# A graph layer: twelve single rows per step instead of twenty-four, fourteen gathers instead of twelve

## The chip, the core and the metric

The kernel runs on one core of a Trainium2 chip. The metric is the device time of one execution in microseconds, less is better. Three executions of the kernel before took 17983.56, 17994.12 and 17994.94 us; the median is 17994.12.

## The reference

One layer of a graph network with two kinds of edges, a residual sum and a layer norm. There are 50000 nodes with 128 features (f32), and 1650000 edges: 800000 random pairs in both directions and one self-loop per node. They are sorted by `dst`; `src` is random.

```python
Xs = X[src]
m_data = Xs @ W_data.T + b_data
m_ctrl = Xs @ W_control.T + b_control
msg = jnp.where((edge_types == 0)[:, None], m_data, m_ctrl)
agg = jax.ops.segment_sum(msg, dst, num_segments=X.shape[0])
out = jax.nn.relu(agg + (X @ W_self.T + b_self))
x = _layernorm(x + out, axis=-1)
```

The matrices can be applied after the sum: per node it is enough to have the sum of its neighbours' rows for each kind of edge, and how many edges of each kind there are.

## The kernel before, in words

**Blocks and steps.** `straight` walks the sorted edges in NBLK = 514 blocks. All blocks but the first and the last hold BE = 3212 edges, in Q = 2 steps of 1606. The edges of a step come in by three ways:

- R = 12 *gathers* of 128 edges (L536). GpSimd issues an indirect DMA, which fetches 128 rows of x, one per partition, into a slot of the tile `y`. Each gather's column of indices is in `idx`.
- F = 46 *fillers*. In the gathers, an edge whose source is its own destination (a self-loop) needs no fetch, since that row is loaded for the block anyway. `columns` counts the loops per gather and ranks them; `fill` (L349 to L378) writes the next filler edges into the places of the loops and makes the new indices. What is left over is passed to the next step (`late`, the serial chain at L323, up to LATE = 10 edges); FX = 56 is F plus these. `by` holds which nodes' loops were taken out; the `left_out_` functions (L380 to L409) build a matrix from it and put the loops' own rows back.
- S = 24 *single rows*. Each is a DMA of its own with one row of 512 bytes, its address in a register (L510); SP issues 12 and ScalarE 12 per step (TURNS), so 48 per block, 24576 in all. They are issued after the first pass of a block, for the block two further on, into the tile `yx`.

The first block and the last have gathers only (24 and 19), so that there are 24 + 512 x 24 + 19 = 12331 gathers.

**Sums.** For each gather, TensorE multiplies the rows in `y` by a 0/1 matrix `oh` (L467, DVE: 128 x 26 columns of 2W = 120; W = 60 is how many nodes a step may span, once for each kind of edge) and adds up in PSUM (`acc`, L555). The matrix of a step's single rows is the thirteenth column (L561). `cnt` (L475, DVE) is the sum of `oh` over the gathers and gives the counts (L564). `add` (L569, DVE) adds a step's `acc` to the block's `sums` at an address in a register, `begin_sums` (L571) takes over the overlap with the block before. `layer` (L582 to L591) multiplies a finished block of B = 112 nodes by the matrices, `moments`, `root` and `store` (L593 to L622) do the norm, and SP writes the rows (L626).

**Order.** The order is written out by hand (`manual_schedule`); every engine works its instructions off in this order, and tiles are given back through semaphores. A block's 24 gathers are four *passes* of PASS = 6. `y` has SLOTS = 10 slots, each for one pass: `gathers` (L530) gives a pass to GpSimd, and TensorE waits until the pass has landed (L543). GpSimd may issue the pass after next ten only when TensorE is done with the slot's last use.

Around the four passes of a block (L682 to L735): ahead of the first pass come `spread` for the block to be filled (L347, TensorE), the add of the last block's second step, `begin_sums`, `onehot` and `counts` for the block two further on (AHEAD). After the first pass come `left_out_columns` (L384, TensorE, reads `by`) and `fill` for a block up to five further on (RAHEAD); after the second the layer of the block before, the loops' rows and the moments; after the third, in the second block of each group of GB = 10, `columns` for the next group.

**Beginning and end.** Ahead of the loop (L661 to L681) the numbers of all blocks (L205 to L223), `columns(0)`, `fill(1)` and `fill(2)` are made. The last block is treated like the others; `find_bad` runs at its beginning and finds out whether the data kept the bounds that the kernel assumes (else a general version runs). After the loop come the last two stores.

Of the kernel before, what the change touches and what calls it, by code (L numbers as in the profile page):

```python
# [12 lines left out]
F32 = mybir.dt.float32  # L13
# [14 lines left out]
P = 128  # L28
# [6 lines left out]
R = 12  # L35
W = 60
Q = 2
PASS = 6
B = 112
C = R * Q  # L40
F = 46
LATE = 10
FX = LATE + F
TURNS = (12, 12)
# [37 lines left out]
GS = GB * Q  # L82
SPAN = 8
# [14 lines left out]
def straight(ctx, tc, c, x, x_t, edges_t, edges_f, src_x, dst_first, first_p, out):  # L98
# [62 lines left out]
    row_of = keep.tile([GB, GB], BF16, name="row_of")  # L161
    nc.vector.tensor_copy(row_of, c["ident"][:GB, :GB])
# [41 lines left out]
    nc.vector.tensor_tensor(begin_p, begin_p, base_p, op=ALU.add)  # L204
    wide = keep.tile([1, WG, SPAN], F32, name="wide")  # L205
    bases_f = keep.tile([1, WG * SPAN], F32, name="bases_f")
    nc.vector.memset(bases_f, float(N - B))
    nc.vector.tensor_copy(bases_f[:, :NBLK], base[0:1, :NBLK, 0])
    first_of_span = bases_f.rearrange("o (w s) -> o w s", s=SPAN)
    nc.vector.tensor_scalar(wide, first_of_span[:, :, 0:1].to_broadcast([1, WG, SPAN]), float(N - WIDE), None, op0=ALU.min)  # L210
    within = keep.tile([1, WG, SPAN], F32, name="within")
    nc.vector.tensor_tensor(within, first_of_span, wide, op=ALU.subtract)
    at_i = keep.tile([1, WG * SPAN, 4], I32, name="at_i")
    nc.vector.tensor_copy(at_i[:, :NBLK, :Q], begin[0:1, :NBLK, :])
    nc.vector.tensor_scalar(at_i[:, :, 3], within.rearrange("o w s -> o (w s)"), 0.0, float(WIDE - B), op0=ALU.max, op1=ALU.min)
    nc.vector.tensor_tensor(begin, begin, base.to_broadcast([P, BL, Q]), op=ALU.add)
    base_i = keep.tile([1, WG, 2 * SPAN], I32, name="base_i")
    nc.vector.tensor_scalar(base_i[:, :, 0], wide[:, :, 0], 4.0, None, op0=ALU.mult)
    nc.vector.tensor_scalar(base_i[:, :, 1:1 + SPAN], first_of_span, float(ROW), None, op0=ALU.mult)
    shift = keep.tile([1, NBLK], F32, name="shift")  # L220
    nc.vector.memset(shift, 0.0)
    nc.vector.tensor_tensor(shift[:, 1:], base[0:1, 1:NBLK, 0], base[0:1, :NBLK - 1, 0], op=ALU.subtract)
    nc.vector.tensor_scalar(at_i[:, :NBLK, 2], shift, 0.0, float(B), op0=ALU.max, op1=ALU.min)  # L223


# [10 lines left out]
    def columns_of(d, t, first, name):  # L236

        rel = eds.tile(list(d.shape), F32, name="rel" + name, bufs=1)
# [3 lines left out]
        nc.vector.tensor_scalar(col, t, 0.0, float(W), op0=ALU.not_equal, op1=ALU.mult)  # L242
        nc.vector.tensor_tensor(col, col, rel, op=ALU.add)
        return col, rel
# [8 lines left out]
    def packed(src, col):  # L253

        lim = eds.tile(list(col.shape), F32, name="lim", bufs=1)
        nc.vector.tensor_scalar(lim, col, 0.0, float(COLS - 1), op0=ALU.max, op1=ALU.min)
        v = eds.tile(list(col.shape), F32, name="v")
        nc.vector.scalar_tensor_tensor(v, src, float(COLS), lim, op0=ALU.mult, op1=ALU.add)
        return v

    def columns(g):
# [27 lines left out]
        col, rel = columns_of(a["d"], a["t"], first_of, "")  # L289
        check(a["d"], rel, [stats[:, 0, m, g:g + 1] for m in range(2)], "")  # L290
        col_f, rel_f = columns_of(a["df"], a["tf"], first_of_f, "_f")
# [5 lines left out]
        with nc.allow_low_precision(reason="whole numbers below 256 times a power of two"):  # L297
            nc.vector.tensor_scalar(v_f[:, 0, :], col_f, 0.0, float(COLS - 1), op0=ALU.max, op1=ALU.min)
            lo = eds.tile([GB, Q * FX], F32, name="lo", bufs=1)
            nc.vector.scalar_tensor_tensor(lo, hi, -float(COLS), a["sf"], op0=ALU.mult, op1=ALU.add)  # L300
            nc.vector.tensor_scalar(v_f[:, 1, :], lo, float(COLS), None, op0=ALU.mult)
            nc.vector.tensor_scalar(v_f[:, 2, :], hi, float(COLS * COLS), None, op0=ALU.mult)

        cb = eds.tile([P, GB, C1], F32, name="cb")
        nc.vector.tensor_scalar(cb, a["t"], 0.0, float(P), op0=ALU.not_equal, op1=ALU.mult)
        nc.vector.tensor_tensor(cb, cb, a["d"], op=ALU.add)
# [8 lines left out]
        more = eds.tile([P, GS], F32, name="more", bufs=1)  # L315
        nc.vector.tensor_scalar(more, rank[:, :, R], -1.0, float(F), op0=ALU.mult, op1=ALU.add)
        late = eds.tile([P, GS + 1], F32, name="late")
        if g == 0:
            nc.vector.memset(late, 0.0)
        else:  # L320
            nc.vector.tensor_copy(late[:, 0:1], late_g[g - 1][:, GS:])
        for k in range(at, n):
            nc.vector.tensor_scalar(late[:, k + 1:k + 2], more[:, k:k + 1], late[:, k:k + 1], 0.0,  # L323
                                    op0=ALU.add, op1=ALU.max)
# [5 lines left out]
        if n < GS and g > 0:  # L330
            nc.vector.memset(late[:, n + 1:], 0.0)
# [8 lines left out]
    def spread(b):  # L340

        if plain(b):
            return
        g, i = divmod(b, GB)
        vf = lists[b % 2][:, :Q * FX]
        for m in range(3):
            nc.tensor.matmul(vf, row_of[:, i:i + 1].to_broadcast([GB, P]), vp_g[g][:, m, :], start=m == 0, stop=m == 2)  # L347
# [71 lines left out]
    def steps_of(b):  # L419
        return [q for q in range(Q) if len(chunks_of(b, q))]  # L420

    def passes_of(b):

        for p in range(C // PASS):
            q = p * PASS // R
            yield q, [k for k in chunks_of(b, q) if k // PASS == p]

# [36 lines left out]
    def onehot(b):  # L464
        g, i = divmod(b, GB)
        oh = ohp.tile([P, C1, 2 * W], F32, name="oh")
        nc.vector.tensor_tensor(oh, col_g[g][:, i, :, None].to_broadcast([P, C1, 2 * W]),  # L467
                                num_ps[:, None, :].to_broadcast([P, C1, 2 * W]), op=ALU.is_equal)
        ohs[b] = oh

    def counts(b):

        cnt = ohp.tile([P, Q, 2 * W], BF16, name="cnt")
        with nc.allow_low_precision(reason="whole numbers up to R1"):
            nc.vector.tensor_reduce(cnt, ohs[b].rearrange("p (q r) w -> p q w r", r=R1), AX.X, ALU.add)  # L475
        cnts[b] = cnt
# [105 lines left out]
    def layer(b):  # L582
        a = sums[b % RING]
# [3 lines left out]
        nc.tensor.matmul(po, xT, c["wselfT"], start=True, stop=False)  # L587
        nc.tensor.matmul(po, a[0:3, 2, :B], bias, start=False, stop=False)  # L588
        for t in range(2):
            nc.tensor.matmul(po, a[:, t, :B], c["wmsgT"][:, t * D:(t + 1) * D], start=False, stop=t == 1)  # L590
        pos[b] = both  # L591

    def moments(b):  # L593
        h = stp.tile([B, D], F32, name="h", bufs=4)
        po = pos.pop(b)
        nc.vector.tensor_copy(h, po[:, 1, :])  # L596
        nc.vector.scalar_tensor_tensor(h, po[:, 0, :], 0.0, h, op0=ALU.max, op1=ALU.add)  # L597
        st = stp.tile([B, 6], F32, name="st")
        nc.vector.bn_stats(st, h)  # L599
        if b % 2 == 0:  # L600
            mvs[b // 2] = stp.tile([B, 2, 2], F32, name="mv")
        mv = mvs[b // 2][:, b % 2, :]
        nc.vector.bn_aggr(mv, st)
        hs[b] = h

    def pair(b):

        return range(b // 2 * 2, b + 1) if b % 2 == 1 or b == NBLK - 1 else ()

    def root(bs):  # L610
        sd = stp.tile([B, 2], F32, name="sd")
        nc.scalar.activation(sd[:, :len(bs)], mvs[bs[0] // 2][:, :len(bs), 1], AF.Sqrt, bias=c["eps"][:B, :])
        sds[bs[0] // 2] = sd

    def store(bs):
        mv = mvs.pop(bs[0] // 2)
        rstd = stp.tile([B, 2], F32, name="rstd")
        nc.vector.reciprocal(rstd[:, :len(bs)], sds.pop(bs[0] // 2)[:, :len(bs)])
# [41 lines left out]

    for b in range(1, AHEAD + 1):  # L661
        offsets(b)
    columns(0)
    window(0)
    spread(1)
    fill(1)
# [3 lines left out]
    onehot(0)  # L670
    counts(0)
# [10 lines left out]
    for b in range(NBLK + 1):  # L682
        if b == NBLK - 1:
            find_bad()
# [5 lines left out]
        due, fresh = fresh, range(made + 1, min(b + RAHEAD, made + 2, NBLK - 1) + 1)  # L690
# [5 lines left out]
        if b < NBLK:  # L696
            begin_sums(b)
# [5 lines left out]
        for q, (step, ks) in enumerate(passes_of(b)):  # L703
# [21 lines left out]
            if q == 2 and i == 1 and g + 1 < GROUPS:  # L725
                columns(g + 1)
# [9 lines left out]
    store(pair(NBLK - 1))  # L736
    for b in (*ready, *pair(NBLK - 1)):
        store_rows(b)
# [338 lines left out]
```

## Time and profile before

| | |
|---|---|
| median of three executions | 17994.12 us |
| the profiled execution | 18008.86 us |
| its span | 18006.8 us |
| GpSimd (POOL) busy | 11686.9 us, 65% |
| VectorE (DVE) busy | 12374.8 us, 69% |
| TensorE matmuls (PE) busy | 8608.7 us, 48% |
| ScalarE (ACT) busy | 79.2 us |
| granted TensorE clock, mean | 0.54 |
| HBM traffic over the span | 50 GB/s |

The span is what the profile records from the first instruction to the last; the profiled execution's own time is 2 us longer, and 15 us above the median of the three executions. A line of a group has the line of the program, the engine, the operation, out<-in with sizes and the number of instructions, then busy time in us and the mean duration in ns, then the idle time of that engine ahead of these instructions, and what ended most of it. A line of the timeline has the start in us, the duration, the instruction, and in brackets the idle time before it and what ended that. Queues (SPq, ACTq, POOLq) are the DMAs that an engine issued. "Remote" is a release that the profile can't put down to an instruction of this core. Idle time of an engine that is not the bottleneck costs nothing.

### The profile page before, as it was taken

What the parts mean: (1) busy time and instruction counts of PE and PEld (TensorE: products, weight loads), DVE (VectorE), ACT (ScalarE), POOL (GpSimd) and SP (SyncE); (2) the same over time, 40 slices, a digit from 0 to 9 for tenths busy, and PEclk for the clock granted to TensorE, in tenths of its full rate; (3) what the DMA queues carried; (4) which work ended last, traced back from release to release, by engine and by line L of the source; (5) the groups of instructions that cost most, each with busy time, mean ns of one, the idle gap of its engine ahead of it and who ended that gap; (6) DMA issues with size and microseconds to landing.
All of it is one profiled execution on the core that took longest, in us unless ns stands there. A gap on an engine that the chain in (4) does not pass through costs nothing.

```text
span 18006.8 us, 165600 instructions
## 1 busy us (share of the span) xinstructions
PE 8608.7 (48%) x37659; PEld 7345.2 (41%) x37660; DVE 12374.8 (69%) x15212; ACT 79.2 (0%) x263; POOL 11686.9 (65%) x12341
## 2 busy tenths in 40 slices
PE   3444444444444444444444444444444444444444
PEld 3344443444344444444444444444444444444444
DVE  7676676676666666666766766676676676667665
ACT  0000000000000000000000000000000000000000
POOL 6666666666666666666666666666666666666666
PEclk6555555555555555555555555555555555555555
DMA  1111111111111111111111111111111111111111
GB/s 52 51 50 51 52 50 51 52 50 51 50 52 51 50 52 50 51 51 51 51 50 52 51 50 51 51 51 51 51 51 50 51 52 50 51 52 50 51 50 48
DMA packets 529272, 913.91 MB, mean 51 GB/s; under 512 B 232762, under 2 KB 315875, under 8 KB 528274
## 3 DMA queue, kind: packets, MB, share of 16 engines
q0 software_dynamic: 394592, 808.89, 15.7%
q1 hardware_dynamic: 108668, 87.80, 1.7%
q10 hardware_dynamic: 25014, 6.54, 0.2%
q8 instruction: 306, 5.01, 0.1%
q14 instruction: 692, 5.67, 0.1%
HBM read 872.82 MB, written 29.47 MB: 50 GB/s over the span
## 4 chain that ended last, share of the span: by engine, by line
DVE 51%; another core or an unknown queue 28%; issue 13%; PE 7%; DVEq 0%; ACTq 0%; ACT 0%
DVE cnt L475 14%; DVE oh L467 8%; PE acc L555 5%; DVE m L358 4%; DVE v_new L365 4%; DVE new L361 4%; DVE old L374 4%; DVE sums L569 2%; DVE late L323 1%; DVE z L392 1%; DVE h L597 1%; DVE st L599 1%; DVE xT L461 1%; DVE h L596 1%
## 5 line engine op out<-in xcount | busy, mean ns | idle before, releaser
L536 POOL DMA_INDIRECT y<-in_x,idx x12312 | 11667.4, 948 | 6272.6 <-issue 3435.2
L555 PEld LDWEIGHTS acc<-oh,y 128*128 128x128 f32 x24662 | 5375.0, 315 | 8665.3 <-issue 8100.0
L555 PE MATMUL acc<-oh,y 128*128 128x120 f32 x24662 | 6002.7, 413 | 3679.8 <-issue 3675.4
L569 DVE TENSOR_TENSOR sums<-acc,sums 128x180 f32 x1028 | 350.0, 340 | 4142.8 <-remote 3960.0
L475 DVE TENSOR_REDUCE cnt<-oh 128x240 bf16<-128x3120 f32 x514 | 3008.2, 5852 | 17.9
L384 PE MATMUL small<-ones_b,by 128*112 128x1 bf16 x512 | 83.5, 164 | 4632.6 <-issue 3934.5
L467 DVE TENSOR_TENSOR oh<-col,small 128x3120 f32<-128x3120 f32 x514 | 1740.8, 3387 | 117.3 <-remote 95.1
L377 DVE TENSOR_REDUCE by<-old 128x112 bf16<-128x1456 f32 x512 | 1427.3, 2788 | 17.4
L358 DVE TENSOR_TENSOR m<-rk,small 128x1456 f32<-128x1456 f32 x512 | 855.7, 1671 | 17.4
L361 DVE TENSOR_TENSOR new<-m,small 128x1456 f32<-128x1456 f32 x512 | 855.2, 1670 | 17.5
L365 DVE TENSOR_REDUCE v_new<-new 128x26 f32<-128x1456 f32 x512 | 855.0, 1670 | 17.5
L374 DVE TENSOR_TENSOR old<-m,small 128x1456 f32<-128x1456 f32 x512 | 852.5, 1665 | 0.0
L561 PE MATMUL acc<-oh,yx 24*128 24x120 f32 x2048 | 758.6, 466 | 61.6 <-issue 61.6
L590 PE MATMUL po<-wmsgT,sums 128*112 128x128 f32 x2056 | 612.8, 453 | 5.5 <-issue 5.5
L561 PEld LDWEIGHTS acc<-oh,yx 24*128 24x128 f32 x2048 | 486.9, 292 | 293.0 <-issue 281.7
L596 DVE COPY h<-po 112x128 f32<-112x128 f32 x514 | 144.8, 282 | 537.1 <-remote 451.3
L590 PEld LDWEIGHTS po<-wmsgT,sums 128*112 128x112 f32 x2056 | 448.4, 297 | 130.7 <-issue 130.0
L347 PE MATMUL small<-v_f,row_of 10*128 10x112 bf16 x1536 | 218.2, 272 | 563.8 <-DVE at L391 168.6
L588 PE MATMUL po<-bias,sums 3*112 3x128 f32 x1028 | 391.5, 482 | 0.2 <-DVE sums L569 0.2
L347 PEld LDWEIGHTS <-row_of 10*128 10x128 bf16 x1536 | 121.7, 112 | 599.5 <-issue 562.2
L587 PE MATMUL po<-wselfT,xT 128*112 128x128 f32 x1028 | 324.9, 420 | 0.0
L564 PE MATMUL acc<-cnt,to_row 128*128 128x60 bf16 x2056 | 281.2, 227 | 13.8 <-issue 13.7
(141 smaller groups left out, 4709.2 us busy)
## 6 DMA issues: line engine op xcount, KB each, us to landing
y<-in_x,idx POOLq DMA_INDIRECT x12312
yx<-in_x SPq DMA_DIRECT2D x12288, 0.5 KB
yx<-in_x ACTq DMA_DIRECT2D x12288, 0.5 KB
xw<-in_x_t SPq DMA_DIRECT2D x65, 448.0 KB
out<-o SPq DMA_DIRECT2D x514, 56.0 KB
sdt<-in_edges_t SPq DMA_DIRECT2D x52, 390.0 KB
one_g<-in_src_x SPq DMA_DIRECT2D x52, 1.9 KB
sdt_f<-in_edges_f SPq DMA_DIRECT2D x52, 13.1 KB
```

Of the source, the lines that this page charges most:

```text
L358: nc.vector.tensor_tensor(m, rk_g[g][:, i, :, None].to_broadcast([P, C1, FX]), rank_no_ps[:, None, :].to_broadcast([P, C1, FX]), op=ALU.is ...
L361: nc.vector.tensor_tensor(new.rearrange("p (q r) f -> p q r f", r=R1), m.rearrange("p (q r) f -> p q r f", r=R1), vf.rearrange("p (q f) -> ...
L365: nc.vector.tensor_reduce(v, new, AX.X, ALU.add)
L374: nc.vector.tensor_tensor(old, m, cb[:, :, None].to_broadcast([P, C1, FX]), op=ALU.mult)
L377: nc.vector.tensor_reduce(by, old.rearrange("p (q r) f -> p q f r", r=R1), AX.X, ALU.add)
L467: nc.vector.tensor_tensor(oh, col_g[g][:, i, :, None].to_broadcast([P, C1, 2 * W]), num_ps[:, None, :].to_broadcast([P, C1, 2 * W]), op=AL ...
L475: nc.vector.tensor_reduce(cnt, ohs[b].rearrange("p (q r) w -> p q w r", r=R1), AX.X, ALU.add)
L536: copy = nc.gpsimd.indirect_dma_start(out=y[:r, k % PASS, :].bitcast(U8), out_offset=None, in_=x_rows, in_offset=bass.IndirectOffsetOnAxis ...
L555: nc.tensor.matmul(acc[:, :2, :].rearrange("p t w -> p (t w)"), y[:r, k % PASS, :], ohs[b][:r, column(k), :], start=k == of_step[0], stop= ...
L561: nc.tensor.matmul(acc[:, :2, :].rearrange("p t w -> p (t w)"), ys[b][:, q, :], ohs[b][:S, q * R1 + R, :], start=False, stop=True)
L569: nc.vector.tensor_tensor(part, accs.pop((b, q)), part, op=ALU.add)
L590: nc.tensor.matmul(po, a[:, t, :B], c["wmsgT"][:, t * D:(t + 1) * D], start=False, stop=t == 1)
```

## The change

The sizes:

| | before | after |
|---|---|---|
| R, gathers per step | 12 | 14 |
| F, fillers per step | 46 | 53 |
| TURNS, single rows per step | 12 + 12 | 6 + 6 |
| PASS, gathers per pass | 6 | 7 |
| W, nodes that a step may span | 60 | 64 |
| B, nodes per block | 112 | 124 |
| edges per block | 3212 | 3714 |
| blocks | 514 | 445 |
| gathers in all | 12331 | 28 + 443 x 28 + 9 = 12441 |
| single rows in all | 24576 | 10632 |

The ten slots of `y` hold seven gathers each. In `columns` the serial chain over the steps of a group becomes two running scans over 21 columns, five adds and five minima, several pairs of operations become one, and the call moves from the second block of a group to the fifth. In the first blocks, the lead of `fill` grows by one block per block instead of two. At the beginning `columns(0)`, `spread(1)` and `fill(1)` come ahead of the block numbers, and `onehot(0)` and `counts(0)` ahead of the loops' rows. At the end the last block has passes of two gathers, `find_bad` runs one block earlier, the layer and the stores of the block before are done before the last block's gathers, the last block's own part of the layer (transposition and self matrix) is done ahead, and the last block is stored by itself.

```diff
-R = 12
-W = 60
+R = 14
+W = 64
-PASS = 6
-B = 112
+PASS = 7
+B = 124
-F = 46
+F = 53
-TURNS = (12, 12)
+TURNS = (6, 6)
...
+    def block_numbers():
...
-        for k in range(at, n):
-            nc.vector.tensor_scalar(late[:, k + 1:k + 2], more[:, k:k + 1], late[:, k:k + 1], 0.0,
-                                    op0=ALU.add, op1=ALU.max)
+        while by <= GS:
+            nc.vector.tensor_tensor(up[:, 1 - i, PAD:], up[:, i, PAD:], up[:, i, PAD - by:PAD + GS + 1 - by], op=ALU.add)
+            by, i = 2 * by, 1 - i
+        total = up[:, i, PAD:]
+        least, by, i = up[:, i, :], 1, 0
+        while by <= GS:
+            nc.vector.tensor_tensor(low[:, i, PAD:], least[:, PAD:], least[:, PAD - by:PAD + GS + 1 - by], op=ALU.min)
+            least, by, i = low[:, i, :], 2 * by, 1 - i
+        nc.vector.tensor_tensor(late, total, least[:, PAD:], op=ALU.subtract)
...
+        of = 2 if b == NBLK - 1 else PASS
+        for p in range(C // of):
+            q = p * of // R
+            yield q, [k for k in chunks_of(b, q) if k // of == p]
...
+    def own_part(b):
         both = ps_o.tile([B, 2, D], F32, name="po")
         po, xT = both[:, 0, :], xTs.pop(b)
         nc.tensor.transpose(both[:, 1, :], xT, c["ident"])
         nc.tensor.matmul(po, xT, c["wselfT"], start=True, stop=False)
+        pos[b] = both
...
+    columns(0)
+    spread(1)
+    fill(1)
+    block_numbers()
     for b in range(1, AHEAD + 1):
         offsets(b)
-    columns(0)
     window(0)
-    spread(1)
-    fill(1)
+    onehot(0)
+    counts(0)
...
+    for b in range(NBLK):
+        if b == NBLK - 2:
+            find_bad()
         if b == NBLK - 1:
-            find_bad()
+            if pair(b - 2):
+                store(pair(b - 2))
+                ready.extend(pair(b - 2))
+            while ready:
+                store_rows(ready.pop(0))
...
-        due, fresh = fresh, range(made + 1, min(b + RAHEAD, made + 2, NBLK - 1) + 1)
+        due, fresh = fresh, range(made + 1, min(b + RAHEAD, made + (2 if b > GB // 2 else 1), NBLK - 1) + 1)
...
+        if b == NBLK - 1:
+            layer(b - 1)
+            moments(b - 1)
+            root(pair(b - 1))
+            own_part(b)
+            store(pair(b - 1))
+            for done in pair(b - 1):
+                store_rows(done)
+            for step, ks in passes_of(b):
+                if ks:
+                    products(b, step, ks)
+                    if step not in steps_of(b)[-1:] and ks[-1] == chunks_of(b, step)[-1]:
+                        add(b, step)
+            break
...
-            if q == 2 and i == 1 and g + 1 < GROUPS:
+            if q == 2 and i == GB // 2 - 1 and g + 1 < GROUPS:
                 columns(g + 1)
```

More of the change, by code (lines that the diff above doesn't have):

```diff
@@ L82 @@
 GS = GB * Q
+PAD = 16
 SPAN = 8
@@ L159, in straight @@
         nc.scalar.dma_start(bias[i:i + 1, :], row_bcast(b, 1))
-    row_of = keep.tile([GB, GB], BF16, name="row_of")
-    nc.vector.tensor_copy(row_of, c["ident"][:GB, :GB])
+    ones_f = keep.tile([P, 1], F32, name="ones_f")
+    nc.vector.memset(ones_f, 1.0)
+    runs = keep.tile([P, 4, PAD + GS + 1], F32, name="runs")
+    nc.vector.memset(runs, 0.0)
+    fills_f = keep.tile([P, 1], F32, name="fills_f")
+    nc.vector.memset(fills_f, float(F))
+    last_f = keep.tile([P, 1], F32, name="last_f")
+    nc.vector.memset(last_f, float(COLS - 1))
+    row_of = keep.tile([GB, 2, GB], BF16, name="row_of")
+    nc.vector.tensor_copy(row_of[:, 0, :], c["ident"][:GB, :GB])
+    nc.vector.tensor_scalar(row_of[:, 1, :], c["ident"][:GB, :GB], float(COLS), None, op0=ALU.mult)
     loads = {}
@@ L236, in columns_of @@
     def columns_of(d, t, first, name):
+        nz = eds.tile(list(d.shape), F32, name="nz" + name, bufs=1)
+        one = ones_f[:d.shape[0], :, None] if len(d.shape) == 3 else ones_f[:d.shape[0], :]
+        nc.vector.scalar_tensor_tensor(nz, t, 0.0, one.to_broadcast(list(d.shape)), op0=ALU.not_equal, op1=ALU.mult)
         rel = eds.tile(list(d.shape), F32, name="rel" + name, bufs=1)
@@ L241, in columns_of @@
         col = eds.tile(list(d.shape), F32, name="col" + name, bufs=1 if name else 2)
[L242 to L244 removed]
+        nc.vector.scalar_tensor_tensor(col, nz, float(W), rel, op0=ALU.mult, op1=ALU.add)
+        return col, rel, nz
     def check(d, rel, at, name):
@@ L314, in columns @@
         n = (min((g + 1) * GB, NBLK - 1) - g * GB) * Q
[L315 to L324 removed]
+        up, low = runs[:, :2], runs[:, 2:]
+        nc.vector.scalar_tensor_tensor(up[:, 0, PAD + 1:], rank[:, :, R], -1.0, fills_f.to_broadcast([P, GS]),
+                                       op0=ALU.mult, op1=ALU.add)
+        if g == 0:
+            nc.vector.memset(up[:, 0, PAD:PAD + 1 + at], 0.0)
+        else:
+            nc.vector.tensor_tensor(up[:, 0, PAD:PAD + 1], late_g[g - 1][:, GS:], late_g[g - 1][:, GS:], op=ALU.max)
+        by, i = 1, 0
+        while by <= GS:
[6 more added lines that the diff above has]
+            least, by, i = low[:, i, :], 2 * by, 1 - i
+        late = eds.tile([P, GS + 1], F32, name="late")
+        nc.vector.tensor_tensor(late, total, least[:, PAD:], op=ALU.subtract)
         late_g[g] = late
@@ L346, in spread @@
         for m in range(3):
-            nc.tensor.matmul(vf, row_of[:, i:i + 1].to_broadcast([GB, P]), vp_g[g][:, m, :], start=m == 0, stop=m == 2)
+            nc.tensor.matmul(vf, row_of[:, min(m, 1), i:i + 1].to_broadcast([GB, P]), vp_g[g][:, m, :], start=m == 0, stop=m == 2)
     def fill(b):
@@ L587, in layer @@
         nc.tensor.matmul(po, xT, c["wselfT"], start=True, stop=False)
+        pos[b] = both
+    def layer(b):
+        if b not in pos:
+            own_part(b)
+        a = sums[b % RING]
+        po = pos[b][:, 0, :]
         nc.tensor.matmul(po, a[0:3, 2, :B], bias, start=False, stop=False)
@@ L735, in straight @@
                 store_rows(ready.pop(0))
-    store(pair(NBLK - 1))
-    for b in (*ready, *pair(NBLK - 1)):
-        store_rows(b)
+    b = NBLK - 1
+    add(b, steps_of(b)[-1])
+    layer(b)
+    moments(b)
+    root(pair(b))
+    store(pair(b))
+    store_rows(b)
 def general(ctx, tc, c, x, src, dst, etype, out):
```

78 lines of the change are left out of this document (35 added, 43 removed).

## Prediction

> **What bounds the kernel now.** I read the page's head first, then the gathers' group in part 5, then GpSimd's timeline over some stretches in mid-run, then the waits.
>
> ```profile
> span 18006.8 us, 165600 instructions
> PE 8608.7 (48%) x37659; PEld 7345.2 (41%) x37660; DVE 12374.8 (69%) x15212; ACT 79.2 (0%) x263; POOL 11686.9 (65%) x12341
> L536 POOL DMA_INDIRECT y<-in_x,idx x12312 | 11667.4, 948 | 6272.6 <-issue 3435.2
> ```
>
> GpSimd issues 12312 gathers plus 19 of the last block, 12331 in all; the gathers' group alone is 11667 us busy and 6273 us idle in front, together 17940 of the 18007 us. So I price the time per gather. DVE has 31% idle, the matmul side half. The timeline shows how the idle time is made (start, duration, idle before and who ended it):
>
> ```profile
> 8998.10 0.95 POOL L536 DMA_INDIRECT y<-in_x,idx  x1 [3.84 <-PE acc L555]
> ...
> 9019.37 0.94 POOL L536 DMA_INDIRECT y<-in_x,idx  x1 [0.31 <-issue]
> 9024.09 0.95 POOL L536 DMA_INDIRECT y<-in_x,idx  x1 [3.78 <-remote]
> ...
> 9037.85 0.95 POOL L536 DMA_INDIRECT y<-in_x,idx  x1 [0.30 <-issue]
> 9041.73 0.95 POOL L536 DMA_INDIRECT y<-in_x,idx  x1 [2.93 <-remote]
> ...
> 9055.49 0.95 POOL L536 DMA_INDIRECT y<-in_x,idx  x1 [0.30 <-issue]
> 9059.25 0.95 POOL L536 DMA_INDIRECT y<-in_x,idx  x1 [2.81 <-DVE old L374]
> ...
> 9073.02 0.95 POOL L536 DMA_INDIRECT y<-in_x,idx  x1 [0.30 <-issue]
> 9076.86 0.95 POOL L536 DMA_INDIRECT y<-in_x,idx  x1 [2.89 <-remote]
> ...
> 9098.12 0.95 POOL L536 DMA_INDIRECT y<-in_x,idx  x1 [0.31 <-issue]
> 9103.11 0.95 POOL L536 DMA_INDIRECT y<-in_x,idx  x1 [4.04 <-remote]
> ```
>
> In a run, one gather starts every 1.25 us ((9019.37-8998.10)/17), 0.95 busy and 0.30 idle. Then GpSimd **stops**. From 8998.10 to 9019.37 there are 18 gathers and the stop behind them is 3.78; the next three runs have 12 gathers and stops of 2.93, 2.81 and 2.89; the last has 18 and a stop of 4.04. Runs are whole passes of six. A straight line through 2.88 at 12 and 3.91 at 18 has a slope of 0.172 us per gather; at no gathers it leaves 0.82, of which 0.30 is the ordinary gap. So a stop costs **0.52 us, and each gather of the run ahead 0.172 us more**. Does that hold for the whole kernel?
>
> ```profile
> POOL y L536 <- remote: 2192.3, 743, 6.7
> POOL y L536 <- DVE old L374: 214.7, 76, 2.9
> POOL y L536 <- PE acc L555: 155.0, 77, 5.2
> ```
>
> These rows (total, times, longest) name 896 stops, 1.74 per block of 514. Idle time above the ordinary gaps is 6272.6 - 12312 x 0.30 = 2579 us; the line gives 12312 x 0.172 + 896 x 0.52 = 2584. It holds, and I use it. What GpSimd waits for at a stop is one of the ten slots of y, given back by TensorE:
>
> ```profile
> 9019.52 0.36 PE L555 MATMUL acc<-oh,y 128*128 128x120 f32 x1 [3.14 <-issue]
> ...
> 9023.74 3.28 PE L555 MATMUL acc<-oh,y 128*128 128x120 f32 x16 [1.74 <-issue]
> ```
>
> Toward the end of a run TensorE does one matmul in several us, waiting for nothing that the profile shows; 0.35 us before GpSimd resumes at 9024.09 it is quick again, 16 matmuls in 3.28 us. So TensorE isn't short of capacity; it is held up as long as gathers are being issued. That hold-up is paid back in the stop.
>
> **The change part by part.** *Gathers.* After: 443 blocks of 28, 28 of the first, 9 of the last, 12441; that is +110, at 1.25 us **+138 us**. At 0.172 each, their share of the stops is +19.
>
> *Passes.* A pass is seven gathers and a block still has four passes; ten slots hold 70 gathers. I keep 1.74 stops per block: 1.74 x 445 = 774 instead of 896, -122 at 0.52: **-63 us**.
>
> *Single rows.* 24576 one-row DMAs become 443 x 24 = 10632. Are they what holds TensorE up?
>
> ```profile
> 9029.50 22.41 SPq L510 DMA_DIRECT2D yx<-in_x  x24
> ...
> 9058.25 18.83 SPq L510 DMA_DIRECT2D yx<-in_x  x24
> 9000.83 43.44 ACTq L510 DMA_DIRECT2D yx<-in_x  x48
> ...
> 9065.34 14.75 ACTq L510 DMA_DIRECT2D yx<-in_x  x22
> 9056.88 0.36 PE L555 MATMUL acc<-oh,y 128*128 128x120 f32 x1 [1.23 <-issue]
> ```
>
> SP issues no row from 9051.91 to 9058.25, ScalarE none from 9044.27 to 9065.34. In that silence TensorE falls into the same single matmuls (9056.88), and the stop at 9059.25 is 2.81. The stop at 9041.73, with most of SP's 24 rows and ScalarE's spell in its run, is 2.93. Not more than 0.12 us per stop is the rows' own; halved, 0.06 x 774 = 46 us at most by this row, and the 2.89 and 2.93 of like runs show that 0.04 is scatter. I take 0. From the other side, if all of 0.172 were the rows' (48 per 24 gathers, then 24 per 28: 0.074), the gain is 0.098 x 12441 = 1220 us. Fewer rows as a loss I can exclude: no engine gets work by it, apart from the gathers already counted.
>
> ```profile
> q0 software_dynamic: 394592, 808.89, 15.7%
> ...
> q10 hardware_dynamic: 25014, 6.54, 0.2%
> ```
>
> The gathers (q0) keep the DMA engines busy 15.7% of the span; ScalarE's 12288 rows of half a KB (q10, 6.54 MB) take 0.2%. The Trainium skill, "DMA: Bandwidth & Descriptors", section "Issuing engines are not separate DMA queues", says that DMAs started from different engines end up interleaved on the same 16 engines. By that rule alone, fewer rows free transfer time for the gathers: at 0.2% for 12288 rows, 13944 rows fewer are worth at most 41 us. The shares speak against even that, since the engines are idle four fifths of the time.
>
> *DVE.* The big groups scale with the tile sizes:
>
> ```profile
> L475 DVE TENSOR_REDUCE cnt<-oh 128x240 bf16<-128x3120 f32 x514 | 3008.2, 5852 | 17.9
> L467 DVE TENSOR_TENSOR oh<-col,small 128x3120 f32<-128x3120 f32 x514 | 1740.8, 3387 | 117.3 <-remote 95.1
> L377 DVE TENSOR_REDUCE by<-old 128x112 bf16<-128x1456 f32 x512 | 1427.3, 2788 | 17.4
> L358 DVE TENSOR_TENSOR m<-rk,small 128x1456 f32<-128x1456 f32 x512 | 855.7, 1671 | 17.4
> L569 DVE TENSOR_TENSOR sums<-acc,sums 128x180 f32 x1028 | 350.0, 340 | 4142.8 <-remote 3960.0
> ```
>
> 3120 elements (26 x 120) become 30 x 128 = 3840, x 1.231; 1456 (26 x 56) become 30 x 63 = 1890, x 1.298. L467 and L475: +2.13 us per block; the four ops like L358 (1.67 each): +1.99; L377: +0.83. **+4.95** on 12374.8/514 = 24.1 us. Period: 18006.8/514 = 35.0 us per block now, 18090/445 = 40.6 then; DVE goes from 69% to 72%. What hides it is the wait of L569 for the sums, 3960 us in all, 7.7 per block. Cost 0; without that cover it would be the third rival.
>
> *columns().* The serial chain at L323 becomes ten scans over 21 columns, and the call moves from block 1 of a group to block 4:
>
> ```profile
> L323 DVE TENSOR_SCALAR late<-more,late 128x1 f32<-128x1 f32 x1024 | 219.5, 214 | 44.7 <-DVE late L323 7.3 <-issue 1.7
> ```
>
> 264 us over 52 groups, 5 us per group, off DVE; the same cover makes that 0. TensorE's L555 goes from 120 to 128 columns, 7% more beside a 48% share: 0.
>
> *Beginning and end.*
>
> ```profile
> 33.80 0.95 POOL L536 DMA_INDIRECT y<-in_x,idx  x1 [0.30 <-issue]
> 46.20 0.95 POOL L536 DMA_INDIRECT y<-in_x,idx  x1 [11.45 <-DVE idx L369]
> 27.29 0.46 DVE L323 TENSOR_SCALAR late<-more,late 128x1 f32<-128x1 f32 x2
> ...
> 37.32 1.96 DVE L323 TENSOR_SCALAR late<-more,late 128x1 f32<-128x1 f32 x8 [1.18 <-DVE late L323]
> 17968.54 0.95 POOL L536 DMA_INDIRECT y<-in_x,sdt  x1 [0.30 <-issue]
> ```
>
> Block 1's gathers wait 11.45 us for idx, behind 12 us of L323 (27.29 to 39.28). Ten scans take the place of 18 of these links, at some 0.2 us of work each, or up to the 1.4 that a link takes with its wait (0.21 + 1.18); the block numbers move behind fill(1), and block 0 has four more gathers, 5 us, as cover: **-11 us** (0 to -11). After the last gather 37 us remain (17969.5 to 18006.8); the early layer of block b-1, shorter passes and the ready transposed part touch its serial chain: **-5** (+5 to -15).
>
> *Sum*, against the profiled execution's 18008.9 (span 18006.8): 138 + 19 - 63 - 11 - 5 = +78, 18087. The median of the runs is 15 less (17994.1): **18072**, +0.4%.
>
> **The rivals.** *The hold-up eases.* If part of 0.172 is the rows', say a tenth to a fifth, that is 214 to 428 us less; and ten slots of 70 gathers may let stops come every third pass: 445 x 4/3 = 593 of them, 94 us less. Any mix: 17,550 to 17,980; with both at their lower ends 18072 - 308 = 17,764. For it: TensorE's own hold-up is of sequencers, and SP and ScalarE run theirs for the rows; against it: the silent run above. The Trainium skill, "Perfetto Trace Analysis", section "Optimization Strategy", says that the same gap coming back on the engine that should be saturated can mean too few buffers for the next tile. By that rule the larger y slots should make the gaps rarer; the trace agrees that a slot is what is waited for, but also shows TensorE late, which more slots only postpone.
>
> *The rows were the cause.* 0.172 falls to 0.074: 18072 - 1220 = about 16,850, and with stops going too, less.
>
> *DVE makes a third stop* (the other side). TensorE takes its instructions in order, and L384 needs `by`, the end of DVE's chain. From one add to the next:
>
> ```profile
> 9000.10 0.33 DVE sums L569
> ...
> 9017.96 0.08 DVE by L377
> 9018.04 5.85 another core or an unknown queue
> ```
>
> Behind L384 stand the next pass's matmuls, so its slot, so GpSimd. That chain, 17.9 us here, gets 4.95 us longer, while two passes get longer by 2 x 1.25 = 2.5: the slack, 5.85 here, shrinks by 2.45. It decides where the slack is below 2.45 us. One more stop per block is 445 x 0.52 = 231 us: 18,303; with DVE itself late for some us in one block in five, up to 18,450. For it: the block shown has only 5.85 us of slack of a mean 7.7, so others have less. Against it: that mean.
>
> *The change doesn't do what it says:* rows weren't on the path, so halving them buys nothing, while the gathers that replace them cost. That is my forecast itself.
>
> **How the numbers follow.** Forecast 0.45 (17,980 to 18,160; of it slower 0.35, within 0.2% 0.09, faster 0.01); hold-up eases 0.27 (faster 0.25, same 0.02); rows the cause 0.06 (faster); third stop 0.22 (slower). About 0.2% (36 us) is what a measurement of this kernel can tell from no change. Faster 0.32, same 0.11, slower 0.57. Left out of the range: the 0.06 below, 0.05 of the easing's low end, 0.06 of the third stop's high end: 17,640 to 18,380. The likeliest case's own range is 17,980 to 18,160.
>
> **What would show it.** Right: L536 and its successor 12432 + 9 times at 0.95; runs of 7, 14 and 21 gathers with stops near 0.82 + 0.172 n (14: 3.2; 21: 4.4); some 774 named stops; DVE 72%; no 11 us wait at the start. Wrong: stops of 14 below 2.9 (the rows had a share), fewer than 650 stops (the longer slots), over 1000 with DVE's `by` or `small` ahead of them (third rival), or a gather that isn't 1.25 us apart.

## The result and the profile after

The kernel after took 17941.5 us (median of 12 runs, 17930.62 to 17957.17), the kernel before in runs beside it 17985.51 (12 runs, 17975.9 to 17995.46): the ratio is 0.9977, with a 95% interval of 0.9969 to 0.9984. Slower by 0.4% was forecast; it is 0.23% faster. The time lies in the range, the sign is wrong.

The profiled execution of after has a span of 17939.1, 67.7 less than before's. The page's head and its groups, in the order of the prediction:

```profile
span 17939.1 us, 130614 instructions
...
PE 7389.9 (41%) x36220; PEld 6299.0 (35%) x36221; DVE 12520.1 (70%) x12696; ACT 69.2 (0%) x229; POOL 11795.6 (66%) x12451
...
L555 POOL DMA_INDIRECT y<-in_x,idx x12432 | 11785.6, 948 | 6102.1 <-issue 3540.2
...
L494 DVE TENSOR_REDUCE cnt<-oh 128x256 bf16<-128x3840 f32 x445 | 2980.8, 6698 | 15.4
L588 DVE TENSOR_TENSOR sums<-acc,sums 128x192 f32 x889 | 313.5, 353 | 3698.9 <-remote 3131.9
```

L555 is the gather, L494 `cnt`, L588 the add. There are 120 gathers more in this group, as long as before, and still 171 us less idle time ahead of them. GpSimd's timeline in mid-run (the first and last gather of each run):

```profile
8997.13 0.95 POOL L555 DMA_INDIRECT y<-in_x,idx  x1 [4.29 <-remote]
...
9022.15 0.95 POOL L555 DMA_INDIRECT y<-in_x,idx  x1 [0.30 <-issue]
9027.42 0.95 POOL L555 DMA_INDIRECT y<-in_x,idx  x1 [4.32 <-remote]
...
9052.46 0.95 POOL L555 DMA_INDIRECT y<-in_x,idx  x1 [0.31 <-issue]
9055.97 0.95 POOL L555 DMA_INDIRECT y<-in_x,idx  x1 [2.56 <-remote]
...
9063.47 0.95 POOL L555 DMA_INDIRECT y<-in_x,idx  x1 [0.30 <-issue]
9067.51 0.95 POOL L555 DMA_INDIRECT y<-in_x,idx  x1 [3.10 <-remote]
```

The runs are of 21, 21 and 7 gathers, whole passes of seven, with stops of 4.32, 2.56 and 3.10 behind them. The waits of GpSimd in after (total, times, longest):

```profile
POOL y L555 <- remote: 1955.5, 579, 5.7
POOL y L555 <- PE acc L574: 314.0, 96, 4.6
```

"DVE old" has gone from the releasers. I counted all stops in both traces. A stop is where two gathers start more than 1.6 us apart, and its time is what lies above the ordinary 1.252 us between two starts:

| | before | after | difference |
|---|---|---|---|
| gathers x 1.252 | 15438 | 15576 | +138 |
| stops, number | 941 | 728 | |
| stops, time above the ordinary gap | 2518.5 | 2320.7 | -198 |
| from the last gather to the end | 38.3 | 32.1 | -6 |

Of the 198, 11 are the wait at the start (46.20 in before), which is gone. So in mid-run the stops lost **187 us**, where the prediction had +19 - 63 = -44. That difference of 143 us is the question.

### The profile page after: what moved, and what is told of

The parts are those of the page before. It is cut to its first block, busy times and chain, and to the rows that moved or that the text cites. A ratio compares the mean times of both kernels' runs of the same rounds, so it can differ in the third digit from the quotient of the medians.

```text
span 17939.1 us, 130614 instructions
## 1 busy us (share of the span) xinstructions
PE 7389.9 (41%) x36220; PEld 6299.0 (35%) x36221; DVE 12520.1 (70%) x12696; ACT 69.2 (0%) x229; POOL 11795.6 (66%) x12451
## 4 chain that ended last, share of the span: by engine, by line
DVE 46%; another core or an unknown queue 25%; issue 19%; PE 9%; DVEq 0%; DMA 0%; ACTq 0%; ACT 0%
DVE cnt L494 12%; DVE oh L486 8%; PE acc L574 7%; DVE m L376 4%; DVE new L379 4%; DVE v_new L383 4%; DVE old L392 4%; DVE sums L588 1%; DVE z L410 1%; PE acc L580 1%; DVE h L621 1%; DVE st L623 1%; DVE xT L480 1%; PE po L615 1%
## 5 line engine op out<-in xcount | busy, mean ns | idle before, releaser
L555 POOL DMA_INDIRECT y<-in_x,idx x12432 | 11785.6, 948 | 6102.1 <-issue 3540.2
L574 PEld LDWEIGHTS acc<-oh,y 128*128 128x128 f32 x24882 | 4828.0, 283 | 9114.7 <-issue 6900.2
L574 PE MATMUL acc<-oh,y 128*128 128x128 f32 x24882 | 5458.9, 379 | 4301.1 <-issue 4288.6
L494 DVE TENSOR_REDUCE cnt<-oh 128x256 bf16<-128x3840 f32 x445 | 2980.8, 6698 | 15.4
L588 DVE TENSOR_TENSOR sums<-acc,sums 128x192 f32 x889 | 313.5, 353 | 3698.9 <-remote 3131.9
L486 DVE TENSOR_TENSOR oh<-col,small 128x3840 f32<-128x3840 f32 x445 | 1842.1, 4140 | 557.4 <-remote 516.4
L395 DVE TENSOR_REDUCE by<-old 128x126 bf16<-128x1890 f32 x443 | 1550.7, 3500 | 15.1
L376 DVE TENSOR_TENSOR m<-rk,small 128x1890 f32<-128x1890 f32 x443 | 941.0, 2124 | 15.5 <-DVE small L374 0.3
L379 DVE TENSOR_TENSOR new<-m,small 128x1890 f32<-128x1890 f32 x443 | 941.0, 2124 | 15.2
L383 DVE TENSOR_REDUCE v_new<-new 128x30 f32<-128x1890 f32 x443 | 940.0, 2122 | 15.2
L392 DVE TENSOR_TENSOR old<-m,small 128x1890 f32<-128x1890 f32 x443 | 937.4, 2116 | 0.0
L580 PE MATMUL acc<-oh,yx 12*128 12x128 f32 x1772 | 600.9, 427 | 63.4 <-issue 59.2
```

Source lines behind the costliest of these rows:

```text
L376: nc.vector.tensor_tensor(m, rk_g[g][:, i, :, None].to_broadcast([P, C1, FX]), rank_no_ps[:, None, :].to_broadcast([P, C1, FX]), op=ALU.is ...
L379: nc.vector.tensor_tensor(new.rearrange("p (q r) f -> p q r f", r=R1), m.rearrange("p (q r) f -> p q r f", r=R1), vf.rearrange("p (q f) -> ...
L383: nc.vector.tensor_reduce(v, new, AX.X, ALU.add)
L392: nc.vector.tensor_tensor(old, m, cb[:, :, None].to_broadcast([P, C1, FX]), op=ALU.mult)
L395: nc.vector.tensor_reduce(by, old.rearrange("p (q r) f -> p q f r", r=R1), AX.X, ALU.add)
L555: copy = nc.gpsimd.indirect_dma_start(out=y[:r, k % PASS, :].bitcast(U8), out_offset=None, in_=x_rows, in_offset=bass.IndirectOffsetOnAxis ...
```

## The experiments

**Theories.** *Rows*: fewer single rows make the stops cheaper or rarer; at 187 us for 13944 rows that would be 0.0134 us per row. *Longer slots*: 70 gathers of lead instead of 60 make stops rarer. *Larger pass and block*: what else the sizes bring. *Edits*: the moved `columns()`, the scans and the two ends.

One thing came unasked: the runs fell on different chips, and most of these don't show the hold-up at all. The kernel before took 15465 to 15467 us on chips 6, 8, 9, 10 and 12, and 18013 and 18033 on chips 13 and 11; the runs of the result, at 17986, had the hold-up too (the number of their chip is not on record). Chip 8 came twice and was the same both times; none of these chips was seen both ways. Whether it is the chip itself or something else about these runs isn't shown. Ratios are against the kernel before on the same chip. Traces of the kernel before exist from the chip of the result alone, so counts of stops are compared across chips.

### Chips without the hold-up

**e1, edits only.**

```diff
 # the kernel after
-R = 14
-W = 64
+R = 12
+W = 60
-PASS = 7
-B = 124
+PASS = 6
+B = 112
-F = 53
+F = 46
-TURNS = (6, 6)
+TURNS = (12, 12)
```

> The kernel after with the sizes of before (12 gathers and 24 single rows per step, 46 fillers, passes of six): only columns(), its place, the lead of fill, the beginning and the end are changed. Against before (17986 us): if these edits are worth only what they take from the two ends, 11 us at the start and 6 at the end, 17968 and as many stops as before (941). If the moved columns() is what made stops rarer in the kernel after, about 100 us less, below 17890, and under 880 stops.

Measured 15462.6 against 15465.8, 0.9998 (0.9989 to 1.0007): on this chip the edits can't be told from nothing, though 17 us less was expected of the two ends. What the chip shows is worth more (its page):

```profile
span 15460.4 us, 165064 instructions
...
L555 POOL DMA_INDIRECT y<-in_x,idx x12312 | 11666.9, 948 | 3754.6 <-issue 3750.0
```

The gathers are as many and as long as in before, but idle time is 3754.6 instead of 6272.6: 0.305 per gather, the ordinary gap alone, not one slot waited for. SP's timeline shows where the hold-up is missing:

```profile
7521.10 8.09 SPq L529 DMA_DIRECT2D yx<-in_x  x24
```

24 rows in 8.09 us, 0.34 each; in before 22.41, 0.93 each. And TensorE's largest wait here, then the same in before:

```profile
PEld acc L574 <- PEq L562: 6933.7, 2001, 8.1
...
PEld acc L555 <- issue: 8100.0, 3295, 16.8
```

TensorE now waits for gathers to land (L562), where in before it stood at "issue", that is, it waited for nothing that the profile shows. The clock isn't the reason: TensorE was granted 0.51 of its full clock here and 0.54 in before.

**e2, e3, e4, rows left out.** Half of before's, all of before's, all of after's:

```diff
 # e2: before
-            n = Q * TURNS[j]
+            n = Q * TURNS[j] // 2
 # e3: before, e4: after; single_rows returns here, and rows_fetched isn't called
+            ys[b] = zero_rows[0]
+        return
```

> The kernel before with half of its single rows never fetched (12288 of 24576 one-row DMAs left out, so these edges are missing from the sums); gathers, blocks and passes as before. Theory of the rows: the 187 us that the stops lost beyond the start came from 13944 rows fewer, 0.0134 us per row, so 165 us less than before, 17820, and each stop 0.1 us shorter. Theory of the longer slots: the rows cost nothing, 17986 within 15 us, stops of 12 gathers still 2.53 us above an ordinary gap.

> The kernel before with no single row fetched at all (the tile of the rows is zero, these edges are missing from the sums, and TensorE has no wait for them). Theory of the rows: 24576 x 0.0134 = 329 us less, 17657. Theory of the longer slots: 17986 within 15 us. If the rows were the cause of the hold-up itself, the stops would vanish: about 15500 to 16000.

> The kernel after with no single row fetched (10632 left out, their edges missing from the sums). Against after (17941): theory of the rows, 10632 x 0.0134 = 142 us less, 17800; theory of the longer slots, 17941 within 15 us and 728 stops as in the kernel after.

Measured 15465.7 (1.0000), 15464.1 (0.9999) and 15587.2 (1.0078). Where there is no hold-up, leaving rows out saved nothing that can be measured, and the test says nothing of chips that have it.

**e5, the kernel after.**

> The kernel after itself, beside the kernel before on the same chip. In the first four runs the kernel before took 15466 us and its gathers ran 1.249 us apart without stops, where it took 17986 with 941 stops earlier. If the chip of this run is again one without the hold-up, the gathers alone decide: 110 more at 1.249 us, +137, less 3 to 5 at the ends: 15600, ratio 1.0087. If it is one with the hold-up, 17941 and a ratio of 0.9977, with some 728 stops.

Measured 15588.2 against 15466.6: **1.0078** (1.0062 to 1.0095). Here the same change is 121.6 us slower: just its gathers, 110 x 1.249 = 137, less the 16 that were forecast for the two ends. (In e1 only 3 of these 16 came out; its gathers are busy 16.6 us longer in all than e2's on the same chip, 11666.9 against 11650.3, and why is open.)

**Repeats.** The chip couldn't be chosen, so the deciding kernels ran again; e9 to e12, e14 to e16 and e17 met chips without the hold-up once more. e12 fetches each row of after twice, e16 puts a small memset behind each gather:

```diff
 # e12: after
+        for j, (eng, dma), to in [(j, e, t) for t in (0, S) for j, e in enumerate(((SP, nc.sync), (ACT, nc.scalar)))]:
 # e16: after
             copy.then_inc(landed[i], 16)
+            nc.gpsimd.memset(pace, 0.0)
```

> As e2_before_rows12: the kernel before with 12288 of its single rows never fetched (their edges are missing). For a chip with the hold-up, since on the chip of e2 there was none. The longer slots alone changed nothing (e8: 950 stops, 0.9999), the sizes together did (e7: 721 stops, 0.9974), so now the rows stand against the larger pass. Theory of the rows: some 840 stops, each 0.1 us shorter than before's (12 gathers: 2.42 instead of 2.53), about 165 us less, ratio 0.991. Theory of the larger pass: 941 stops, same lengths, ratio 1.000.

> As e3_before_norows: the kernel before without any single row (24576 left out). On a chip with the hold-up, theory of the rows: 330 us less, ratio 0.982; theory of the larger pass: 1.000; if SP's and ScalarE's row instructions were the cause of the hold-up itself, the stops vanish: 15500, ratio 0.86.

> As e4_after_norows: the kernel after without any single row (10632 left out). On a chip with the hold-up, against after at 0.9977 of before: theory of the rows, another 142 us less, 0.990; theory of the larger pass, 0.9977 and 728 stops.

> The kernel after with each single row fetched twice, the second time into partitions that nothing reads: 24 row DMAs per step as before, with the gathers, blocks and passes of after. On a chip with the hold-up: theory of the rows, 142 us more than after, ratio 1.0056, stops of 14 gathers 0.1 us longer (2.8 instead of 2.70); theory of the larger pass, as after, 0.9977. On a chip without it, as after there, 1.0078.

> As e10_before_norows: the kernel before without any single row (24576 left out). e13 gave 169 us for 12288 rows, 0.0137 us per row. On a chip with the hold-up: if rows cost in proportion, 24576 x 0.0137 = 337 us less, ratio 0.981; if the rows are the cause of the hold-up itself, most of the 2500 us of stops go, ratio under 0.90; if the first half of the rows was the dear one, 0.988 to 0.991. On a chip without it, 1.000.

> As e11_after_norows: the kernel after without any single row (10632 left out). On a chip with the hold-up, at 0.0137 us per row 146 us less than after's 0.9977: ratio 0.9896; at nothing per row 0.9977. On a chip without it, 1.0079.

> The kernel after with a two-column memset of GpSimd's own behind each gather, which puts some 0.1 to 0.2 us between gathers (GpSimd's smallest memsets took 0.10 to 0.12 us at the start of before's trace). If the hold-up comes from gathers issued faster than something behind them takes them (1.41 us each by the stops' slope), the added time comes out of the stops: on a chip with the hold-up the time stays within 100 us of after. If each gather costs the others a fixed 0.16 us whatever its distance, the added time is paid in full: 12441 x 0.1 = 1240 us or more on top. On a chip without the hold-up it is paid in full in any case.

> As e14_before_norows, once more for a chip with the hold-up: no single row is fetched. In proportion to e13: 337 us less, ratio 0.981. If the rows are the hold-up's cause: under 0.90. If the second half of the rows costs nothing: 0.991. On a chip without the hold-up 1.000.

Measured: e9 0.9999, e10 0.9999, e11 1.0079, e12 1.0080, e14 0.9999, e15 1.0079, e17 0.9999. e16 took 15675.1, 1.0137, which is 87 us or 7 ns per gather above after on such chips, where 1240 us or more were expected: nearly all of the memset, 0.12 us each, lies in the 0.30 us gap. What it would do to the hold-up stays open.

### Chips with the hold-up

**e7, sizes only.** The kernel before with the twelve lines of e1's diff turned round.

> The kernel before with the sizes of after (14 gathers, 12 single rows, 53 fillers, passes of seven) and with its own columns(), beginning and end. On a chip without the hold-up: 110 gathers more, 15466 + 137 = 15603 less what a shorter last block saves. On a chip with it: if the sizes made stops rarer (longer slots or fewer rows), 17960 and some 730 stops; if the moved columns() did, 18090 and over 770 stops.

Measured 17970.0 against 18012.7: **0.9974** (0.9963 to 0.9985), with 721 stops. Within the intervals that is the whole effect of the change (0.9977). The theory of the edits falls.

**e8, longer lead alone.**

```diff
 # before
-SLOTS = 10
+SLOTS = 12
```

> The kernel before with 12 slots of y instead of 10, that is 72 gathers of lead instead of 60 (the kernel after has 70); nothing else. On a chip with the hold-up: theory of the longer slots, some 730 stops instead of 941 and a time 100 to 180 us less; theory of the rows, 941 stops and the same time. On a chip without it, the same time, since no slot is waited for.

Measured 18011.9 against 18012.7: 0.9999 (0.9989 to 1.0008). Its gathers and its largest wait:

```profile
L536 POOL DMA_INDIRECT y<-in_x,idx x12312 | 11666.4, 948 | 6277.6 <-issue 3427.3
```

```profile
POOL y L536 <- remote: 2426.5, 836, 5.0
```

Idle time is 6277.6, in before 6272.6; I count 950 stops. Two more slots buy nothing: the theory of the longer slots falls.

**e13, half the rows.** The same kernel as e2, on a chip with the hold-up (ratio of that chip's own before).

> As e9_before_rows12, again for a chip with the hold-up: the kernel before with 12288 of its single rows never fetched (their edges are missing). Theory of the rows: 165 us less, ratio 0.991, some 840 stops, stops after 12 gathers 2.42 instead of 2.53 above an ordinary gap. Theory of the larger pass and block: ratio 1.000, 941 stops, 2.53. On a chip without the hold-up 1.000 once more, which tells nothing.

Measured 17863.9 against 18032.8: **0.9907** (0.9890 to 0.9923), 169 us less (interval 139 to 198), where the rows' theory had 165. The edit takes away 12288 row DMAs with the register loads of their addresses, and TensorE's matmul of a step's rows reads 12 rows instead of 24: 0.0137 us per row. GpSimd's timeline shows how (first and last of each run):

```profile
9022.33 0.94 POOL L536 DMA_INDIRECT y<-in_x,idx  x1 [3.91 <-remote]
...
9043.55 0.94 POOL L536 DMA_INDIRECT y<-in_x,idx  x1 [0.30 <-issue]
9048.34 0.94 POOL L536 DMA_INDIRECT y<-in_x,idx  x1 [3.84 <-remote]
...
9062.08 0.94 POOL L536 DMA_INDIRECT y<-in_x,idx  x1 [0.30 <-issue]
9065.80 0.94 POOL L536 DMA_INDIRECT y<-in_x,idx  x1 [2.78 <-remote]
...
9094.53 0.94 POOL L536 DMA_INDIRECT y<-in_x,idx  x1 [0.30 <-issue]
9100.01 0.94 POOL L536 DMA_INDIRECT y<-in_x,idx  x1 [4.54 <-remote]
```

18, 12 and 24 gathers, with stops of 3.84, 2.78 and 4.54. Runs of four passes, which are eight in all of before, are common here. Counted over the whole traces (number of runs, median of the stop behind them above the ordinary gap):

| run of | before | e13 | after |
|---|---|---|---|
| one pass | 154, 1.54 | 127, 2.56 | 115, 2.27 |
| two passes | 468, 2.53 | 190, 2.37 | 175, 2.70 |
| three passes | 306, 3.47 | 332, 3.49 | 389, 3.85 |
| four passes | 8, 4.48 | 135, 4.49 | 29, 4.91 |
| all stops | 941 | 788 | 728 |

By the medians a stop behind three or four passes is as long with half the rows as with all; behind two passes it is 0.16 shorter, behind one pass 1.02 longer. What changes most is **how far a run gets**: without half of the rows GpSimd gets a pass or two further before it stands, and 153 stops fewer are made. After has the same picture with passes of seven.

The number of stops also accounts for the time. A straight line through all stops of before against the length of their runs (without the wait at the start) is 0.86 us per stop and 0.138 per gather. With these two numbers the stops of before, e13 and after should take 2513, 2381 and 2345 us in all; 2518, 2398 and 2321 were counted. e7 and e8 fit as well (2339 and 2520; 2334 and 2523). So one price holds for all five within about 1%, and the kernels differ in how often GpSimd stops. Between the spans of before and e13 lie 147 us: 120 are stops, 22 are ordinary gaps that are 2 ns shorter, 5 the end. How a row ends a run is not shown. TensorE's timeline in e13 shows that the hold-up itself is still there:

```profile
9013.56 0.36 PE L555 MATMUL acc<-oh,y 128*128 128x120 f32 x1 [2.46 <-issue]
9015.69 0.36 PE L555 MATMUL acc<-oh,y 128*128 128x120 f32 x1 [1.77 <-issue]
9018.49 0.36 PE L555 MATMUL acc<-oh,y 128*128 128x120 f32 x1 [2.44 <-issue]
9020.59 0.36 PE L555 MATMUL acc<-oh,y 128*128 128x120 f32 x1 [1.74 <-issue]
9021.99 3.20 PE L555 MATMUL acc<-oh,y 128*128 128x120 f32 x15 [1.04 <-issue]
```

Single matmuls 2 to 3 us apart up to 9021.99, then 15 in 3.20 us as GpSimd is about to resume (9022.33). With half of the rows 788 of 941 stops are left, and the chips without the hold-up fetch just as many rows, so the rows alone don't make the hold-up. Whether it would be there with no rows at all wasn't seen, since e3, e10, e14 and e17 met other chips.

The Trainium skill, "DMA: Bandwidth & Descriptors", section "Issuing engines are not separate DMA queues", has DMAs of all engines interleave on the same engines; by that the prediction bounded the rows' transfer time at 41 us. 169 were measured, for fewer rows, with the gathers' queue at 17.9% of the DMA engines' time in e13. By that sum, shared transfer time isn't what the rows cost here.

**e6, the other way.**

```diff
 # the kernel of e1
-TURNS = (12, 12)
-LOADS = 1
+TURNS = (30, 30)
+LOADS = 2
```

> The opposite of the change's direction: the kernel after with the sizes of before (12 gathers, 46 fillers, passes of six), but with 60 single rows per step instead of 24 (30 on SP and 30 on ScalarE, fetched in two parts). 503 blocks, 12061 gathers, 270 fewer than the kernel before. On a chip without the hold-up SP took 0.34 us per row, so 60 rows of a block are 20 us beside a block of 30, hidden, and the gathers decide: 15463 - 270 x 1.249 = 15126, ratio 0.978. On a chip with the hold-up, where SP took 0.93 us per row, 60 rows are 56 us beside a block of 35: SP becomes the bound, over 25000; if rows lengthen stops only by 0.0134 us each, 18000.

Measured 22604.9 against 18012.7: 1.2546 (1.2525 to 1.2567). The group of the rows' matmuls and SP's timeline:

```profile
L580 PE MATMUL acc<-oh,yx 60*128 60x120 f32 x2004 | 630.7, 406 | 13596.3 <-PEq L538 12969.1 <-issue 627.2
```

```profile
9032.89 42.23 SPq L529 DMA_DIRECT2D yx<-in_x  x60
9075.29 0.34 SPq L655 DMA_DIRECT2D out<-o  x1
```

TensorE waits 12969 us for rows (L538 is their semaphore). SP needs 42.23 us for 60, 0.70 each; I had expected 0.93 and over 25000. As a bound on SP the direction was right, the size too high. The Trainium skill, "DMA: Bandwidth & Descriptors", section "Issuing engines are not separate DMA queues", says that the time an engine's sequencer takes to start a DMA is usually small relative to the DMA itself. How long the DMA of one row takes was not measured here; but with 60 rows to issue in a block of 44.9 us, 0.70 us each, issuing them was the bound.

### More rows where there is no hold-up

**e19, 36 rows per step**, the kernel of e6 with TURNS = (18, 18). The same with the rows fetched in one part (e18) gave no result.

> As e6_rows60, but with 36 single rows per step (18 on SP and 18 on ScalarE, fetched in two parts): 510 blocks, 12240 gathers, 91 fewer than before, and 36576 rows, 12000 more. On a chip without the hold-up, where the rows cost nothing beside the gathers: 15463 - 91 x 1.249 = 15349, ratio 0.9925, faster than both kernels there. On a chip with it: rows at 0.0137 us +164, gathers at 1.41 us -129, ends -17: the same time within 0.2%; if SP with 0.93 us per row (33 us of a block of 35) is already the bound, over 1.02.

It met chip 12, without the hold-up: 15352.2 against 15465.8, **0.9927** (0.9910 to 0.9943), where 0.9925 was expected. Each row more saves 1/128 of a gather, and on this chip nothing took that back:

```profile
L555 POOL DMA_INDIRECT y<-in_x,idx x12216 | 11571.7, 947 | 3727.1 <-issue 3722.1
```

There this version beats both kernels. On a chip with the hold-up it wasn't run; at 0.0137 us per row and 1.41 per gather I estimate no difference there.

## Why the prediction was wrong, point by point

- **The gathers** are right: +110 at 1.252, 138 us. 0.948 us each as before.
- **Single rows at 0: this step failed.** The prediction said "Not more than 0.12 us per stop is the rows' own" and took 0. It compared the length of two stops behind runs of 12, one with rows issued and one without. But the rows decide how far a run gets more than how long the stop behind it is (e13), and a comparison at equal run length can't see that. Its own sign of a share, "stops of 14 below 2.9", would have missed it too: 2.70 + 0.30 = 3.0 was measured. What the runs showed in place of 0 is 169 us for 12288 rows; in proportion, an estimate, the 13944 rows of the change are worth 191 (158 to 225).
- **The first rival** ("the hold-up eases", a tenth to a fifth of 0.172, 214 to 428 us) named the rows and came close to the size: 191 is 9% of 0.172 x 12441. Its mechanism is not what the runs show: it let each gather cost less, while the medians in the table still rise by 0.15 to 0.19 us per gather from two passes on, with all the rows or half of them. So its size is in part luck.
- **Passes, -63.** The reason given, 1.74 stops per block whatever the size, doesn't stand by itself: counted over the whole trace, before has 1.83 stops per block, e13 1.53, after 1.64. The price was too low as well: at 0.86 instead of 0.52, 1.83 stops per block would make it -108. With the rows' 191 the sum would be 138 + 19 - 63 - 191 - 16 = -113, too much; without the -63 it is -50, beside -68 between the spans and -44 between the medians. So the two amounts don't add. What a pass of seven does alone was not measured on a chip with the hold-up. Nearest to it are e13 and after, which both fetch 24 rows per block: by their ratios the larger sizes cost some 126 us, where gathers and ends make 138 - 16 = 122. That leaves about nothing for the passes and the gathers' share of the stops together, within some 30 us; by the count, 60 stops fewer at 0.86, they would save 52 less 15. The term stays open.
- **The longer slots**, part of the first rival: nothing (e8).
- **The price of a stop** fits roughly at these two lengths: 0.82 + 0.172 n was 3.2 at 14 and 4.4 at 21 of idle time; measured 2.70 + 0.30 = 3.0 and 3.85 + 0.30 = 4.15. It was read from five stops; through all of them the line leans more on the stop (0.86) and less on the gather (0.138).
- **DVE** is right: 70% busy (72% forecast), `cnt` 6.70 us instead of the scaled 7.20. A third stop per block, the rival on the slower side, didn't happen.
- **The start** is right: -11. Its reason can be seen in DVE's timeline of after: the five adds and five minima take 2.1 us in place of 12, though the wait that a link had in before was not shown to be gone in general.

```profile
20.70 1.07 DVE L336 TENSOR_TENSOR runs<-runs 128x21 f32<-128x21 f32 x5
21.81 1.04 DVE L341 TENSOR_TENSOR runs<-runs 128x21 f32<-128x21 f32 x5
```

- **The end** is right: -6 (forecast -5).
- **"The change doesn't do what it says"** was put as the forecast itself. It holds on the chips without the hold-up, where rows cost nothing and the change is 0.78% slower (e5), and not on the chip that was asked about.

## What to carry to other kernels

Where an engine runs in bursts that end in a stop, a suspected cause has to be tested on both: how long the stop is, and how long the burst before it gets; a pair of equal bursts shows only the first. Ahead of pricing a wait that no instruction explains, ask whether it belongs to the kernel or to the chip it ran on: here a trade of gathers for row DMAs has one sign with the hold-up and the other without.

## What the runs showed of the hardware

I had not expected that the same program takes 15466 us on five chips and 17986 to 18033 on others, each within 0.1%. The gathers are equally long (0.946 to 0.948 us) and their packets equally many; what differs is how fast TensorE, SP and ScalarE work through instructions while gathers are being issued (24 rows on SP in 8.09 or 22.41 us, 48 on ScalarE in 17.87 or 43.44). Why is open. Where it occurs, this kernel pays 1.25 us per gather, 0.14 more for its share of the stops, 0.86 per stop, and 0.0137 for each 512-byte DMA on SP or ScalarE, mostly by way of the stops, though TensorE waits for none of these rows in before.
